# Rounding a weight block by block, and a wider spacing of the last ternary layers, in a two-layer gated cross-attention kernel

## The chip, the cores and the metric

The kernel runs on one core of a Trainium2 chip, in one launch. The metric is the device time of one execution in microseconds; the figure of a kernel is the median of its runs. The core has five engines that run side by side and wait for each other through semaphores: PE (matrix products and transposes), DVE (vector), ACT (scalar functions), POOL (general vector work) and SP, whose queue issues all transfers here. Results of PE lie in PSUM banks until DVE or ACT has read them.

## The reference

The input `x` is 4 batches of 512 rows of 512, `ctx_2048` has the same shape. Each stage adds a gated term to `x`, and each starts from a layer norm of the current `x`:

```python
x = x + tanh(g_xattn[0]) * wkv(w, u, layernorm(x), ctx_2048)      # a recurrence along the rows
x = x + tanh(g_ffn[0])   * ffn(layernorm(x), w1, w2, w3)          # weights sign(w)*mean|w|, inputs int8 in groups of 64
x = x + tanh(g_xattn[1]) * attention(layernorm(x), ctx_2048, ...) # 16 heads; wq, wp and rows int8
x = x + tanh(g_ffn[1])   * ternary(layernorm(x), gamma, W)        # W rounded to -1, 0, 1; rows int8
```

Int8 here means for a weight row: `s = max(max|row| / 127, 1e-8)`, and `round(row / s)` clipped to plus and minus 127. The ternary weight is `round(W / (mean|W| + 1e-5))`, clipped to plus and minus 1. The ternary layer's rows pass a layer norm, then a root of a mean square, gamma, and an int8 rounding by their largest magnitude.

## The kernel before, in words

The four batches go through the four stages one behind the other, and the stages of neighbouring batches run beside each other: while batch b's FFN or attention keeps PE busy, batch b+1's recurrence (`wkv_layer`) fills DVE, ACT and POOL, and batch b-1's ternary layer goes between. Everything is cut into generators, and each `yield` ends a step. `line` (L1239) gives a generator a place in time for its steps, in batches and slots (a batch is 17 slots; in the first, `at_unit(n)` counts sixteenths of the FFN), and `run` always takes the step with the smallest place. A `line` with `(start, end, n)` spreads n steps evenly; an `event` is a single step.

That order alone does not settle the program. PE's instructions keep it from turn to turn: `in_turn` ties every product to the last one of the turn before, `next_turn` ends a turn, and within a turn a scheduler may shift. On DVE, ACT, POOL and SP the scheduler places instructions as it finds them ready in its own estimate, so that an earlier place of a step shifts rows of other steps too. Each engine then runs its list strictly in order.

In the first batch the weights are prepared beside FFN (`class Weights`). `load` fetches a weight of 512 x 512 as four blocks of 128 rows into `wn` (two buffers). For the attention's `wq` and `wp`, `rounded` (L407) takes the largest magnitudes of all four blocks in one instruction (`absmax`, L249), the scales and their reciprocals (`int8_scale`, L259 and L260), and then rounds each block with three instructions (`quantise`, L253 to L255: scale, clip and add a large constant, subtract it), into `wi`. For the ternary weight, `ternary_sums` (L421) sums magnitudes, and `ternary` (L430) forms the mean on PE and rounds the four blocks. `ints_turned` then transposes a weight on PE into PSUM (`wt_ps`, sixteen transposes, four to a bank) and copies it out on DVE and ACT in turn. `output_scales` (L448) turns the scales of `wp` into a row on PE (`pb_ps`), multiplies by the gate on DVE (`swp_b`, L457) and fetches and scales the output bias. In the first batch's PSUM, two banks of tag `m` serve all transposes and batch 3's keys and values (`k_ps`, `v_ps`), so a bank that DVE has not yet read holds up PE.

In the stage around it, FFN's unit on PE is: a product `ff_hp`, a second `ff_hp`, a product `ff_acc`, and four transposes `tp_ps`. Between these stand DVE's L761, L765 (gate), L249, L691, L693, L695 (group rounding) and L712 (`hr`), ACT's L760, L699 and L711, and POOL's L700.

Batch 2's ternary layer lies beside batch 3's attention, and batch 3's is the very end. For both, `statistics` (L1130) takes the moments of the rows and forms the inverse root by a seed and three Newton steps: `rsqrt` on DVE (eleven small instructions, L185 to L195), or `rsqrt_aside`, with the seed on DVE (L202, L204) and twelve instructions on POOL (L209 to L213). Batch 3's tiles go in two pairs, (0, 1) and (2, 3); before the change the first pair's root is formed on DVE and the second's on POOL. `ternary` (L1147) then does for a tile: `tf_xn` (L1158), its largest magnitude (L249), the scales (L1162 to L1176), the rounding on ACT (L264), four transposes (`qr_ps`), a copy to `tf_xT` (ACT L271), four products `f_ps`, and the sum into `xb` (DVE L1189) and out. `tf_xn` has three buffers (tag `ff_a`) for four tiles, so that the fourth waits for the first's transposes. Attention's unit (one head pair, 256 rows) on PE is: two `s_ps`, `o_ps`, eight transposes `pt_ps`, two `s_ps`, eight `pt_ps`, and `ot_ps`; on DVE four maxima (L962), two copies `at_PT` (L982), a reciprocal and `at_o` (L1022).

## Time and profile before

| | us |
|---|---|
| median of 3 runs | 1123.73 (1122.61 to 1124.41) |
| the profiled execution | 1121.98 |
| its span | 1120.2 |
| busy: PE, DVE, ACT, POOL | 960.3, 886.3, 711.5, 297.8 |
| mean granted PE clock | 0.954 |

The page lists busy times of each engine, the span in 40 slices, the transfers, the chain of work that ended last, and groups of instructions by line with the engine's idle time before them and what ended it. A row of a timeline gives start, duration, engine, line, operation, output and inputs, and in brackets the idle time before it and who ended that. Rows of one engine overlap by a little, so the time from one start to the next is what an instruction costs in a row of others. PE's clock is granted between 0.5 and 1.0 of full speed, and it shows in the duration of the same product in different places.

### The profile page before, as it was taken

The page shows a single profiled execution, that of the slowest core. Times are in us where ns is not written, and L with a number is a line of the kernel's source. Part 1 is how long each engine was busy: PE and PEld are TensorE (multiplying, and loading weights), DVE is VectorE, ACT ScalarE, POOL GpSimd, SP SyncE. Part 2 cuts the span into 40 slices and gives each one's busy share as a digit, 9 for nine tenths or more (in the row PEclk, how much of TensorE's full clock was granted, in tenths as well). Part 3 has the DMA queues.
Part 4 walks back from the last instruction along what each step waited for, and adds up shares of the span by engine and source line. Part 5 has one row for each costly group of instructions (what it writes and reads, how often), then busy time and mean ns, then how long its engine had stood idle before and what let it go on. Part 6 is the DMA issues. An engine that isn't in the chain of part 4 may idle for free.

```text
span 1120.2 us, 16509 instructions
## 1 busy us (share of the span) xinstructions
PE 960.3 (86%) x5520; PEld 678.2 (61%) x5548; DVE 886.3 (79%) x1884; ACT 711.5 (64%) x1454; POOL 297.8 (27%) x301
## 2 busy tenths in 40 slices
PE   3879898978878978899998797999999899788983
PEld 3345565555546756677776475777777677555651
DVE  5887447778877799998759899977689766689866
ACT  5657655453214677667768676687676677887762
POOL 3822014333104143541215536212122400100000
PEclk8889999998888999999999999999999899999997
DMA  8188953544434664654655555464564563243401
GB/s 281 39 274 321 322 203 129 178 169 153 148 122 151 224 191 157 200 178 163 205 188 184 164 168 181 142 220 157 181 227 156 181 201 110 89 134 109 123 11 38
DMA packets 85668, 189.58 MB, mean 169 GB/s; under 512 B 12240, under 2 KB 36816, under 8 KB 74576
## 3 DMA queue, kind: packets, MB, share of 16 engines
q1 hardware_dynamic: 85584, 188.53, 50.2%
q8 instruction: 44, 0.72, 0.3%
q14 instruction: 40, 0.33, 0.1%
HBM read 148.65 MB, written 39.85 MB: 168 GB/s over the span
## 4 chain that ended last, share of the span: by engine, by line
PE 46%; DVE 28%; ACT 12%; issue 5%; DMA 5%; POOL 3%; SPq 1%; POOLq 0%; ACTq 0%; DVEq 0%
PE ff_hp L168 13%; PE ff_acc L168 6%; PE pt_ps L171 6%; PE o_ps L168 4%; PE v_ps L168 3%; PE s_ps L168 3%; DVE wk_q L655 3%; DVE at_nm L962 3%; ACT at_P L964 3%; PE k_ps L168 2%; PE tp_ps L171 2%; DVE qg_i L695 2%; PE qr_ps L171 1%; ACT at_PT L984 1%; DVE ff_z L765 1%
## 5 line engine op out<-in xcount | busy, mean ns | idle before, releaser
L168 PE MATMUL ff_hp<-wT,xp 128*128 128x512 f32 x1024 | 270.5, 408 | 3.3 <-ACT at_P L964 2.1
L168 PEld LDWEIGHTS ff_hp<-wT,xp 128*128 128x128 f32 x1024 | 194.3, 193 | 51.3 <-ACT at_P L964 4.4
L964 ACT ACTIVATE at_P<-s_ps,at_nm 128x512 f32<-128x512 f32 x256 | 174.5, 689 | 61.8 <-DVE at_nm L962 61.4
L962 DVE TENSOR_REDUCE at_nm<-s_ps 128x1 f32<-128x512 f32 x256 | 166.0, 677 | 28.4 <-PE s_ps L168 28.0
L700 POOL TENSOR_TENSOR ff_z<-qg_b,qg_s 128x512 f32<-128x512 bf16 x64 | 71.1, 1111 | 381.1 <-ACT qg_b L699 328.4
L171 PE MATMUL pt_ps<-ident,at_P 128*128 128x128 f32 x1024 | 141.3, 278 | 11.7 <-ACT at_os L1004 5.2
L984 ACT COPY at_PT<-pt_ps 128x512 f32<-128x512 f32 x224 | 124.7, 595 | 38.1 <-PE pt_ps L171 37.5
L171 PEld LDWEIGHTS pt_ps<-ident,at_P 128*128 128x128 f32 x1024 | 113.2, 141 | 53.1 <-issue 13.8
L168 PE MATMUL ff_acc<-wT,hr 128*128 128x512 f32 x512 | 136.6, 408 | 6.3 <-DVE hr L712 3.3
L168 PE MATMUL s_ps<-at_kR,at_qR 128*128 128x512 f32 x256 | 98.1, 449 | 21.9 <-ACT at_P L964 14.6
L168 PEld LDWEIGHTS ff_acc<-wT,hr 128*128 128x128 f32 x512 | 92.4, 190 | 27.3 <-DVE hr L712 4.6
L760 ACT ACTIVATE ff_z<-ff_hp,coef 128x512 f32<-128x512 f32 x64 | 43.9, 686 | 67.2 <-PE ff_hp L168 65.2
L168 PE MATMUL o_ps<-at_PT,at_V 128*32 128x256 f32 x1024 | 72.0, 395 | 1.3 <-DVE hr L712 0.7
L699 ACT CAST qg_b<-qg_i 128x512 bf16<-128x512 int8 x80 | 49.4, 618 | 36.7 <-DVE qg_i L695 24.6
L168 PE MATMUL v_ps<-wkvT,cT 128*128 128x512 f32 x128 | 65.9, 664 | 5.3 <-DVE wT L336 2.3
L765 DVE SCALAR_TENSOR_TENSOR ff_z<-ff_hp,coef,ff_z 128x512 f32<-128x512 f32 x64 | 47.6, 744 | 27.9 <-PE ff_hp L168 27.8
L168 PEld LDWEIGHTS s_ps<-at_kR,at_qR 128*128 128x128 f32 x256 | 45.7, 193 | 39.4 <-ACT at_P L964 23.8
L761 DVE SCALAR_TENSOR_TENSOR ff_z<-ff_z,ff_hp 128x512 f32<-128x512 f32 x64 | 43.4, 679 | 24.2 <-ACT ff_z L760 24.0
L168 PE MATMUL k_ps<-cT,wkvT 128*128 128x512 f32 x128 | 59.3, 613 | 3.1 <-ACT cT L479 1.4
L711 ACT CAST hr<-tp_ps 128x512 fp32r<-128x512 f32 x64 | 37.6, 587 | 35.7 <-PE tp_ps L171 35.7
L655 DVE RECIPROCAL wk_q<-wk_q 128x256 f32<-128x256 f32 x32 | 54.3, 1718 | 1.4 <-POOL wk_p L643 1.4
L171 PE MATMUL tp_ps<-ident,ff_z 128*128 128x128 f32 x256 | 41.2, 286 | 14.4 <-ACT at_PT L984 5.3
(190 smaller groups left out, 1735.7 us busy)
## 6 DMA issues: line engine op xcount, KB each, us to landing
wT<-wD SPq DMA_DIRECT2D x72, 1024.0 KB, 5.2
wn<-in_L_ffn_w_dram SPq DMA_DIRECT2D x18, 1024.0 KB, 6.8
at_kR<-kD SPq DMA_DIRECT2D x128, 128.0 KB, 3.0
at_qR<-qD SPq DMA_DIRECT2D x256, 64.0 KB, 2.2
wD<-wT SPq DMA_DIRECT2D x12, 1024.0 KB, 5.0
kD<-k_half SPq DMA_DIRECT2D x16, 512.0 KB, 3.3
qD<-at_half SPq DMA_DIRECT2D x32, 256.0 KB, 2.1
cn<-in_ctx_dram SPq DMA_DIRECT2D x8, 512.0 KB, 5.9
```

What stands on the lines that cost most here:

```text
L168: return in_turn(nc.tensor.matmul(*args, **kwargs))
L171: return in_turn(nc.tensor.transpose(*args))
L655: nc.vector.reciprocal(half, half)
L699: nc.scalar.copy(qb, qi)
L700: nc.gpsimd.tensor_tensor(grouped(src), grouped(qb), s.unsqueeze(2).to_broadcast([P, NG, GS]), ALU.mult)
L711: nc.scalar.copy(part[:, 0, :], pt)
L760: nc.scalar.activation(z, hp, AF.Tanh, scale=coef[:, 0:1])
L761: nc.vector.scalar_tensor_tensor(z, z, 1.0, hp, ALU.add, ALU.mult)
L765: nc.vector.scalar_tensor_tensor(z, hp, coef[:, 1:2], z, ALU.mult, ALU.mult)
L962: nc.vector.tensor_reduce(nm, sp, AX.X, ALU.max, negate=True)
L964: nc.scalar.activation(lanes[k, i, t], sp, AF.Exp, bias=nm, accum_out=sums[k][:, t, i : i + 1],)
L984: made[k] = nc.scalar.copy(dst, blocks(pt))
```

## The change

Six edits, in two places of the program. In the first batch: `rounded` takes each block's maximum, scale and reciprocal by itself, rounds the block, and ends a step there; `ternary` ends a step after each rounded block; their steps are spread over 0.6 to 0.8 units, starting 0.2 units earlier; the transposes start 0.05 units later; and `output_scales` comes at unit 13.75 instead of 14.7. In the last batches: the fourth tile's `tf_xn` takes a buffer of the recurrence (`wk_o`); the two pairs of batch 3 exchange the engines of their roots; and the seven steps of batch 2's ternary layer spread over 9.8 slots instead of 7.

```diff
         def rounded(self, key):
...
-            absmax(am, wn)
...
-            int8_scale(s, r, am)
-            wi = self.pool.tile([P, NC, D], BF16, name="wi", tag="sg", bufs=2)
+            self.ints[key] = wi = self.pool.tile([P, NC, D], BF16, name="wi", tag="sg", bufs=2)
             for j in range(NC):
-                quantise(wi[:, j, :], wn[:, j, :], r[:, j : j + 1], -127.0)
-            self.ints[key] = wi
+                at = slice(j, j + 1)
+                absmax(am[:, at], wn[:, j, :])
+                int8_scale(s[:, at], r[:, at], am[:, at])
+                quantise(wi[:, j, :], wn[:, j, :], r[:, at], -127.0)
+                yield
...
             for j in range(NC):
                 quantise(wi[:, j, :], wn[:, j, :], rf, -1.0, 1.0)
-            self.ints["f"] = wi
+                yield
...
-        y = rsqrt_aside(v, n) if b == NB - 1 and tiles[0] else rsqrt(v, n)
+        y = rsqrt_aside(v, n) if b == NB - 1 and not tiles[0] else rsqrt(v, n)
...
-            xn = ff.tile([P, D], F32, name="tf_xn", tag="ff_a", bufs=3)
+            if t == NT - 1:
+                xn = wk.tile([P, T + 1], F32, name="tf_xn", tag="wk_o")[:, 0:D]
+            else:
+                xn = ff.tile([P, D], F32, name="tf_xn", tag="ff_a", bufs=3)
...
-                event(at_unit(load + 1.2), made.ternary)
+                line(made.ternary(), (at_unit(load + 1.0), at_unit(load + 1.6), 4))
             else:
-                event(at_unit(load + 1.0), lambda key=key: made.rounded(key))
-            line(made.ints_turned(key), (at_unit(load + 1.6), at_unit(load + 2.4), 4))
-        event(at_unit(14.7), made.output_scales)
+                line(made.rounded(key), (at_unit(load + 0.8), at_unit(load + 1.6), 4))
+            line(late(lambda key=key: made.ints_turned(key)), (at_unit(load + 1.65), at_unit(load + 2.45), 4))
+        event(at_unit(13.75), made.output_scales)
...
-                else (end + 4.85 / SLOTS, end + 11.85 / SLOTS, 7),
+                else (end + 4.85 / SLOTS, end + 14.65 / SLOTS, 7),
```

The built order of the changed kernel differs from the old one in three stretches of DVE, PE and ACT: the rounding of the three weights, batch 2's ternary layer, and the end. DVE has 18 instructions more (six maxima, six scales, six reciprocals); no engine has any other in number.

More of the change, by code (lines that the diff above doesn't have):

```diff
@@ L438, in ternary @@
             nc.vector.reciprocal(rf, mf)
-            wi = self.pool.tile([P, NC, D], BF16, name="wi", tag="sg", bufs=2)
+            self.ints["f"] = wi = self.pool.tile([P, NC, D], BF16, name="wi", tag="sg", bufs=2)
             for j in range(NC):
                 quantise(wi[:, j, :], wn[:, j, :], rf, -1.0, 1.0)
-            self.ints["f"] = wi
+                yield
         def ints_turned(self, key):
```

## The prediction

> **What bounds the kernel now.** I read the page first (PE 86% of the span, DVE 79%; the chain of work that ended last is PE 46%, DVE 28%, ACT 12%), then placed the edits: the weights' rounding (rows of `w_am`, `wn`, `wi`) runs from 238.7 to 318 us, batch 2's ternary layer from 1017.8 to 1057 us beside batch 3's attention, and the last pairs from 1092 us to the end. In each I read the windows, PE's waits, and the timelines of PE and DVE. PE's waits between 228 and 350 us (us in total, times, longest):

> ```profile
> PE wt_ps L171 <- DVE swp_b L457: 5.1, 1, 5.1
> PE wt_ps L171 <- DVE k_half L291: 4.3, 3, 3.6
> PE tp_ps L171 <- DVE wT L336: 3.5, 1, 3.5
> ```

> All three wait for DVE: the first while twelve instructions of `ternary` stand in a row (313.40 to 317.84), the second behind the whole-tile maximum, the third behind rounding. Three DVE rows of this stage (start, duration):

> ```profile
> 238.70 2.29 DVE L249 TENSOR_REDUCE w_am<-wn 128x4 f32<-128x2048 f32 x1 [0.62 <-DMA wn<-in_L_xattn_wq_dram]
> 271.39 0.42 DVE L254 TENSOR_SCALAR wn<-wn 128x512 f32<-128x512 f32 x1
> 276.07 1.45 DVE L254 TENSOR_SCALAR wn<-wn 128x512 f32<-128x512 f32 x1
> ```

> The first is what is cut in four. The other two are one instruction, 0.42 us alone and 1.45 us beside POOL's `wk_q` L650 (275.15 to 277.23). Batch 2's ternary layer, on PE and in the windows (PE, PEld, DVE, ACT, POOL busy, clock):

> ```profile
> 1031.05 0.93 PE L171 MATMUL qr_ps<-ident,tf_xn 128*128 128x128 f32 x4 [2.75 <-ACT tf_xn L264]
> ...
> 1032.76 1.94 PE L168 MATMUL o_ps<-at_PT,at_V 128*32 128x256 f32 x16
> ...
> 1039.52 1.07 PE L168 MATMUL o_ps<-at_PT,at_V 128*32 128x256 f32 x16
> ```

> ```profile
> 1020.00:1030.00 10.00, 7.14 (x56) 4.86 (x54) 10.00 (x36) 7.82 (x21) 0.00 (x0) 1.00 0.47 137
> 1040.00:1050.00 10.00, 9.79 (x81) 6.60 (x75) 8.04 (x15) 7.86 (x21) 0.00 (x0) 1.00 0.47 146
> ```

> PE stands 2.75 us before the first tile's transposes, with attention's next unit queued behind, while DVE is full; after it `o_ps` takes 1.94 us instead of 1.07. The end:

> ```profile
> 1103.41 0.19 POOL L209 TENSOR_TENSOR rs_t<-ln_v,rs_y 128x2 f32<-128x2 f32 x1 [137.65 <-DVE rs_y L204]
> ...
> 1106.49 0.19 POOL L213 TENSOR_TENSOR rs_y<-rs_y,rs_t 128x2 f32<-128x2 f32 x1
> ```

> ```profile
> 1107.41 0.81 ACT L264 ACTIVATE tf_xn<-tf_xn,magic,tf_s 128x512 f32<-128x512 f32 x1 [1.92 <-DVE tf_s L1171]
> 1108.13 1.24 ACT L271 ACTIVATE tf_xT<-qr_ps,magic 128x512 bf16<-128x512 f32 x2
> ```

> POOL's roots of the second pair take 3.3 us; ACT's rounding of that pair waits for them, and the first pair's copies `tf_xT` stand behind it.

> **Part 1, rounding (forecast -2.5 us).** The order of instructions of the two kernels, from the first `w_am` to the last `wi`, is priced by start-to-start time between neighbours that wait for nothing: reduce or copy of 512 elements 0.60, `L253` 0.40, `L254` and `L255` 0.34, scan 1.14, half reciprocal 1.66, small ones 0.07 to 0.11. Before, this gives 65.5 us of the 79.1 between 238.70 and 317.84; idle rows add 0.90+0.33+1.42+2.39+1.11+1.27+0.19+0.21 = 7.8; the other 5.8 are mostly rows stretched beside POOL (L695 1.20, L660 1.31, L255 1.21, L647 1.77, L254 1.45, L193 1.00: 4.9 over their usual).

> Added: eight maxima of 0.60 for two of 2.20 (+0.4), twelve more scales and reciprocals (+0.9). Moved ahead of the end: `swp_b` (+0.66) and one `hr` (+0.60); behind it, one batch-norm row and small ones (-0.9). So 67.2. What is saved is idle time, as PE's feeders on DVE (`k_half`, `wT`, `hr`) stand earlier. At 251.77 PE waits for `k_half` with 1.6 us less ahead of it. PE's `tp_ps` of 282.15 comes some 4 us sooner by hand: the rows between the scan at 271.73 and the `wT` copy that it waits for come to 4.6 us instead of 6.5, and the scan stands 1.9 sooner. So the 2.39 us that DVE idles behind a `v_ps` at low clock (6.71 us for 3.45; granted 0.72 from 285 to 295) goes, and I take 1.3 from the smaller ones. Idle 4.1, stretched rows as before: 238.7 + 67.2 + 5.8 + 4.1 = 315.8. PE's `wt_ps` of 318.63 needs no `swp_b` any more: 316.0, 2.6 sooner, rounded to 2.5. What is late next: `wpT`'s transposes. By the order, the third weight's sums (2.20) stand ahead of the second's last block, so PE waits some 4 us near 293, a wait that before lacks. Ends: no idle at all, 311.7, PE at 311.9 (-6.7); idle as before and eight more stretched rounding rows (two of 36 before, 0.92 over each, 7.3), 326.8, PE at 327.0 (+8.4).

> From 345 us to 1017 us PE, DVE and ACT have the same order in both, so I carry the shift. Costed at nothing: the load of batch 3's `xb` on SP passes behind a `kD` and a `wD` store (278.68, 279.14, 282.07) and lands 6.6 us after issue; the first FFN of batch 1 hides it, else 3.4 us. One POOL memset (0.10) changes places with an `ff_z`; ACT's `wk_xn` passes one copy; `bp_b`'s load and product stay early in both orders.

> Row first: L254 0.42 alone, 1.45 beside POOL. [...]

> **Part 2, batch 2's ternary layer (forecast -3.0 us).** Steps stand 1.4 slots apart instead of 1.0, and the fourth tile has a row of its own. PE's units (starts of their first `s_ps`: 1022.32, 1031.63, 1038.77, 1044.96, 1051.16, 1056.91, 1062.35, 1067.67, 1073.43) take 9.31, 7.14, 6.19, 6.20, 5.75, 5.44, 5.32, 5.76. DVE's part of a unit is 4x0.60 + 2x0.60 + 0.3 = 3.9; a tile adds 0.65 + 0.60 + 0.4, later 0.67. Before, three tiles and the roots stand ahead of the second unit's maxima (1032.60). After, two do (1.9 less), and the transposes of the first stand behind that unit's scores: PE goes from `ot_ps` (end 1028.1) straight on, 3.5 us sooner. Then DVE has 2.0 to 2.3 us beside its 3.9 in two units, and PE 1.3 us of transposes and products in three: by hand the seven units are 6.35, 5.4, 5.9, 6.3, 6.6, 5.4, 6.2, together 42.15, so 1028.1 + 42.15 = 1070.25 where before has 1073.43: 3.2 sooner. I take 3.0, as the third and fourth tile stand together on DVE. Ends: the whole wait and the slow rows behind it (0.87+0.49+0.32), -4.4; DVE is full to 1041 either way, so 0, or +1 if the two tiles hold up a unit.

> **Part 3, the end (forecast -0.5 us).** First pair on POOL: seed at 1097.90, twelve POOL instructions 3.3, so 1101.3 instead of DVE's 1103.25. But DVE, in order, stands from 1099.6 to 1101.3, and the second pair's statistics wait behind. First rounding on ACT at 1102.0 (before 1103.98), second pair's `ln_v` done 1103.8 (before 1101.7). Its roots on DVE have two `xb` L1189 in their midst, which wait for `f_ps`: the second's end lies at 1107.5 with PE at full clock, at 1108.4 with half. Nine steps less three already done at 0.2, then 0.7 of scales: ACT's rounding at 1110.0 to 1111.0. Before, PE had f_ps until 1112.45 and the tail followed at 3.6 to the last `xb`. From 1110.0 at full clock 4.1 give 1114.1 (-1.9); from 1111.0 at half clock 6.4 give 1117.4 (+1.3). PE stands some 2.5 us before it, and 2.75 at 1028 sufficed for slow rows, so I stay near the middle: -0.5.

> **Sum.** -2.5 - 3.0 - 0.5 = -6.0. The profiled execution took 1121.98 (span 1120.2), so 1116.0; it lies 1.75 under the median of the runs shown, 1123.73, and against that the forecast is **1117.7**.

> **Rivals.** *DVE was the bound in the rounding all along*: idle time only changes places. For it: DVE is 76 to 100% busy in every window from 245 to 315. Part 1 gives 0, time 1120.2. Chance 0.18.

> *Stretched rows*: the roundings strewn beside POOL's products of `wkv_layer` (1.26 to 2.14 each, ten between 244 and 281) stretch by 0.92, eight more than before, on FFN's own path, so that no idle goes: part 1 +8.4, with the rest +4.9, time 1128.6, slower. It decides from a loss over 3.5 + 2.25 us in part 1. Against it: before, two of 36 met. Chance 0.14.

> *Part 2 gives nothing*, DVE being full there in either order, and part 1 half: 1122.0. Chance 0.10.

> *PE keeps its clock* between 270 and 330, near both ends of parts 1 and 2: -6.7 - 4.4 - 0.5 = -11.6, 1112.1. Chance 0.08.

> Forecast as summed, between 1114 and 1120: 0.50.

> **Chances.** 0.2% (2.25 us) is about what a measurement of this kernel can tell from no change. Faster takes the forecast, the clock case and most of the first rival: 0.69. Same takes its rest and the third: 0.16. Slower: 0.15. The range for 8 in 10 runs from 1111.5 to 1126.5; outside are the worse part of the stretched rows and a little of the clock case.

> **What would show it.** Part 1: the `wt_ps` wait of 5.1 under 4.5 and the attention's first `qr_ps` (348.60) near 346; a new wait before `wpT`'s transposes. Part 2: no wait of 2.75 before the first `tf_xn` transposes, the unit after 1022 near 6 instead of 9.3. Part 3: POOL's twelve at about 1098 relative to before, DVE idle 1.7 us, the first pair's `tf_xT` two to four us sooner. Wrong: L253 to L255 rows of 1.2 us in number, a new PE gap near 293 over 6 us, or DVE idle as long as before.

## The result, and the profile after

The changed kernel takes **1125.32 us** (median of 22 runs, 1120.24 to 1127.76); the kernel before, on the same chip, 1122.63 us (22 runs, 1116.02 to 1127.99). The ratio is 1.0026 (95% interval 1.0015 to 1.0038): slower by some 3 us, where 6 us less were forecast. The profiled execution took 1126.90 us, its span is 1125.1, its mean granted clock 0.951.

First the rounding. PE's waits of the changed kernel between 228 and 350 us (us in total, times, longest), to be held against the three of before:

```profile
PE wt_ps L171 <- DVE wi L255: 7.7, 5, 2.0
PE tp_ps L171 <- DVE wT L336: 2.8, 1, 2.8
PE wt_ps L171 <- DVE k_half L291: 2.8, 1, 2.8
```

The one long wait for `swp_b` (5.1) is gone, those for `k_half` and `wT` are shorter (4.3 and 3.5 before), and five waits for rounded blocks, 7.7 us together, are new. Two of the five stand before the second weight's transposes. Rows of DVE and, below, of PE in that place:

```profile
296.44 2.28 DVE L428 TENSOR_REDUCE w_part<-wn 128x64 f32<-128x2048 f32 x1
298.63 0.42 DVE L255 TENSOR_SCALAR wi<-wn 128x512 bf16<-128x512 f32 x1
...
300.60 0.43 DVE L255 TENSOR_SCALAR wi<-wn 128x512 bf16<-128x512 f32 x1
```

```profile
299.11 0.23 PE L171 MATMUL wt_ps<-identb,wi 128*128 128x128 bf16 x1 [1.97 <-DVE wi L255]
301.09 0.23 PE L171 MATMUL wt_ps<-identb,wi 128*128 128x128 bf16 x1 [1.75 <-DVE wi L255]
```

The third weight's sums (`w_part`, 2.28 us) run on DVE ahead of the second weight's last two blocks, and PE stands 3.7 us for these. The other three waits (4.0 us) stand before the third weight's transposes. On DVE the stretch from the first `w_am` to the last `wi` takes 79.6 us (before 79.2), with 7.2 us idle (before 8.0); the same list of instructions takes 81.4 us, 8.8 of them idle, in the profile of the rounding edits alone. Two of the rounding rows are stretched beside POOL (1.20 and 1.07 us), as two were before.

Batch 2's ternary layer, PE rows and two windows (PE, PEld, DVE, ACT, POOL busy, clock):

```profile
1037.77 0.50 PE L168 MATMUL s_ps<-at_kR,at_qR 128*128 128x512 f32 x1 [0.98 <-ACT at_P L965]
1038.10 0.60 PE L171 MATMUL qr_ps<-ident,tf_xn 128*128 128x128 f32 x4
...
1042.02 1.07 PE L168 MATMUL o_ps<-at_PT,at_V 128*32 128x256 f32 x16 [1.35 <-ACT at_PT L985]
```

```profile
1020.00:1030.00 10.00, 8.88 (x72) 5.47 (x73) 9.84 (x28) 7.10 (x19) 0.00 (x0) 1.00 0.70 194
1040.00:1050.00 10.00, 8.48 (x75) 5.44 (x74) 9.55 (x26) 8.09 (x20) 0.00 (x0) 1.00 0.11 31
```

PE no longer stands before the first tile's transposes (2.75 us before), and is busier from 1020 to 1030 (8.88 of 10 us, before 7.14); from 1040 to 1050 it is less busy (8.48, before 9.79), since waits of about 1 us for ACT's `at_P` and `at_PT` come instead. The changed program stands 5.4 us later here; windows shifted by that (1025.4 to 1035.4, 1045.4 to 1055.4) have 9.04 and 8.33. The units from the third's first `s_ps` to the start of the last one's `o_ps` take 60.3 us, before 61.9.

The end, rows of POOL, DVE and ACT:

```profile
1101.78 0.20 POOL L209 TENSOR_TENSOR rs_t<-ln_v,rs_y 128x2 f32<-128x2 f32 x1 [130.47 <-DVE rs_y L204]
...
1105.28 0.20 POOL L213 TENSOR_TENSOR rs_y<-rs_y,rs_t 128x2 f32<-128x2 f32 x1
```

```profile
1105.51 0.33 DVE L1166 TENSOR_SCALAR tf_s<-tf_s,rs_y 128x1 f32<-128x1 f32 x2 [2.03 <-POOL rs_y L213]
```

```profile
1106.21 1.52 ACT L264 ACTIVATE tf_xn<-tf_xn,magic,tf_s 128x512 f32<-128x512 f32 x2 [9.55 <-DVE tf_s L1175]
...
1114.54 1.52 ACT L264 ACTIVATE tf_xn<-tf_xn,magic,tf_s 128x512 f32<-128x512 f32 x2 [4.77 <-DVE tf_s L1175]
```

POOL takes 3.7 us, DVE stands 2.03 us for it (before, 2.58 us for the second pair's), and ACT rounds the second pair 8.3 us after the first. From the last unit's `o_ps` to the end of the span it is 42.3 us, before 41.2.

The profile after thus has -1.7 us in the rounding, up to attention's second `qr_ps` (349.73 before, 349.52 after), -1.6 in the units and +1.1 at the end. The rest of its 4.9 us lies where the programs are the same: 1.5 ahead of the first edit, and 5.6 between that `qr_ps` and the units in batch 3's attention (first `s_ps` 1017.10 before, 1022.49 after). Whether the change does that, or the execution that was profiled, the two traces cannot say.

### The profile page after: what moved, and what is told of

Its sections match the earlier page's. It is cut to its first block, busy times and chain, and to the rows that moved or that the text cites. A ratio compares the mean times of both kernels' runs of the same rounds, so it can differ in the third digit from the quotient of the medians.

```text
span 1125.1 us, 16520 instructions
## 1 busy us (share of the span) xinstructions
PE 965.0 (86%) x5520; PEld 682.7 (61%) x5548; DVE 888.2 (79%) x1902; ACT 711.5 (63%) x1454; POOL 297.8 (26%) x301
## 4 chain that ended last, share of the span: by engine, by line
PE 47%; DVE 27%; ACT 14%; issue 5%; DMA 4%; POOL 3%; SPq 0%; ACTq 0%; POOLq 0%; DVEq 0%
PE ff_hp L168 14%; PE ff_acc L168 6%; PE pt_ps L171 6%; PE s_ps L168 4%; PE o_ps L168 4%; ACT at_P L965 4%; PE v_ps L168 3%; DVE wk_q L656 3%; DVE at_nm L963 2%; DVE qg_i L696 2%; PE k_ps L168 2%; PE tp_ps L171 2%; ACT at_PT L985 2%; PE qr_ps L171 2%; PE f_ps L168 2%
## 5 line engine op out<-in xcount | busy, mean ns | idle before, releaser
L168 PE MATMUL ff_hp<-wT,xp 128*128 128x512 f32 x1024 | 275.6, 413 | 2.8 <-ACT at_P L965 2.1
L168 PEld LDWEIGHTS ff_hp<-wT,xp 128*128 128x128 f32 x1024 | 198.7, 197 | 52.1 <-ACT at_P L965 4.6
L171 PE MATMUL pt_ps<-ident,at_P 128*128 128x128 f32 x1024 | 142.8, 280 | 10.3 <-ACT at_os L1005 4.9
L171 PEld LDWEIGHTS pt_ps<-ident,at_P 128*128 128x128 f32 x1024 | 114.7, 142 | 51.2 <-issue 15.2
L168 PE MATMUL ff_acc<-wT,hr 128*128 128x512 f32 x512 | 138.9, 413 | 6.2 <-DVE hr L713 4.0
L168 PE MATMUL s_ps<-at_kR,at_qR 128*128 128x512 f32 x256 | 99.2, 452 | 22.5 <-ACT at_P L965 15.7
L168 PEld LDWEIGHTS ff_acc<-wT,hr 128*128 128x128 f32 x512 | 94.2, 193 | 27.1 <-DVE hr L713 5.0
L168 PE MATMUL o_ps<-at_PT,at_V 128*32 128x256 f32 x1024 | 70.8, 389 | 2.0 <-ACT at_PT L985 2.0
L168 PEld LDWEIGHTS s_ps<-at_kR,at_qR 128*128 128x128 f32 x256 | 46.0, 194 | 40.2 <-ACT at_P L965 25.2
L168 PE MATMUL v_ps<-wkvT,cT 128*128 128x512 f32 x128 | 64.0, 648 | 5.5 <-DVE wT L336 2.3
L168 PE MATMUL k_ps<-cT,wkvT 128*128 128x512 f32 x128 | 59.9, 618 | 3.1 <-ACT cT L480 1.4
L171 PE MATMUL tp_ps<-ident,ff_z 128*128 128x128 f32 x256 | 39.8, 278 | 14.7 <-ACT at_PT L985 4.9
```

The lines of the kernel that those rows point to most:

```text
L168: return in_turn(nc.tensor.matmul(*args, **kwargs))
L171: return in_turn(nc.tensor.transpose(*args))
```

## The experiments

Two theories to begin with. *Middle*: the rounding edits bring the loss behind 350 us. *Tail*: that loss is scatter, and the exchanged roots make the kernel slower. Ratios are to the kernel before, with 95% intervals; us are these ratios times 1123.3.

**Each part alone.** *Roots alone*:

```
-        y = rsqrt_aside(v, n) if b == NB - 1 and tiles[0] else rsqrt(v, n)
+        y = rsqrt_aside(v, n) if b == NB - 1 and not tiles[0] else rsqrt(v, n)
```

> The kernel before with the exchanged roots alone: last batch's first pair on POOL, second pair on DVE; the program is the same up to some 1092 us. Theory 'middle' (the changed kernel's loss is the 5.7 us that its trace loses between 350 and 1011 us, brought by the rounding edits, and the end adds about what its trace shows): the end, from the last o_ps to the end of the span, is 42.3 us instead of 41.2, time +0.5 to +1.5 us against the kernel before. Theory 'tail' (the 5.7 us are scatter of one execution, the exchange is what makes the kernel slower): +3 to +6 us.

Measured 1.0022 (1.0005 to 1.0038), +2.5 us, in neither theory's range. The end takes 42.6 us, 1.4 more than before. And its profile loses 5.1 us between the same second `qr_ps` and the units, where it is the program of before to the instruction: so two profiles of one program differ by 5 us there.

*Spacing alone*, with the fourth tile's buffer:

```
-                else (end + 4.85 / SLOTS, end + 11.85 / SLOTS, 7),
+                else (end + 4.85 / SLOTS, end + 14.65 / SLOTS, 7),
```

> The kernel before with the wider spacing of batch 2's ternary layer and the fourth tile's own row buffer alone. Both theories: from the third unit's first s_ps to the last o_ps 60.3 us as in the changed kernel instead of 61.9, time -1 to -2 us against the kernel before. If the gain of 1.6 us seen there comes from the other start of the stage and not from the spacing: 0.

Measured 0.9993 (0.9975 to 1.0012), -0.8 us. The units take 60.3 us, 1.6 less, as in the changed kernel; the end takes 42.1 us, 0.9 more. So about half of what the units gain is given back at the end.

*Rounding edits alone*, all that the diff has in the first batch:

```
+                line(made.rounded(key), (at_unit(load + 0.8), at_unit(load + 1.6), 4))
...
+        event(at_unit(13.75), made.output_scales)
```

> The kernel before with the rounding edits alone: block by block in four steps, sooner, output scales at 13.75. Theory 'middle': PE's first ff_hp after wfT's transposes comes 1 to 2 us sooner than before (relative to the stage's start), and 4 to 6 us are lost between 350 and 1011 us: +2 to +4 us against the kernel before. Theory 'tail': the gain of 1.5 us stays, -1 to -2 us.

Measured 1.0033 (1.0015 to 1.0051), +3.7 us. *Rounding edits and spacing*, which is the change without this line:

```
+        y = rsqrt_aside(v, n) if b == NB - 1 and not tiles[0] else rsqrt(v, n)
```

> The changed kernel with the roots as before (rounding edits and spacing together). Theory 'middle': +1 to +2.5 us against the kernel before. Theory 'tail': -2 to -4 us.

Measured 1.0027 (1.0009 to 1.0046), +3.0 us; with the exchanged roots, which is the whole change, +2.9. So the loss is the rounding edits' in all three, the *tail* theory falls, and beside the spacing the exchange costs nothing that can be told. Why it measured +2.5 by itself stays open.

**Which of the rounding edits.** New pair of theories: *late blocks* (the second weight's last block behind the third's sums) against *strewn* (more instructions between others). *wq and wp in steps alone*:

```
-                event(at_unit(load + 1.0), lambda key=key: made.rounded(key))
+                line(made.rounded(key), (at_unit(load + 0.8), at_unit(load + 1.6), 4))
```

> Of the rounding edits, those to wq and wp alone: both block by block in four steps, their transposes 0.05 units later; the ternary weight and the output scales as before. Theory 'late blocks' (the blockwise rounding gains some 2 us up to the first weight's transposes, and gives them back before the second weight's, as the second's last block now stands behind the third's sums of 2.28 us on DVE and PE waits 3.7 us for wi there): the 3.7 us stand in PE's waits, the 5.1 for swp_b too, time +2 to +4 us against the kernel before. Rival 'strewn' (eighteen more instructions, and roundings stretched between others, cost it wherever they stand): +1.5 to +2.5 us, with no change if the 3.7 us wait is absent.

Measured 1.0016 (0.9995 to 1.0037), +1.8 us, which is in the range of *strewn* and just under that of *late blocks*; the two waits stand (wi 3.7, swp_b 4.5). *The ternary weight in steps, output scales at 13.75, alone*:

```
-                event(at_unit(load + 1.2), made.ternary)
+                line(made.ternary(), (at_unit(load + 1.0), at_unit(load + 1.6), 4))
...
-        event(at_unit(14.7), made.output_scales)
+        event(at_unit(13.75), made.output_scales)
```

> Of the rounding edits, the ternary weight in four steps and the output scales at 13.75 alone; wq and wp as before, so that no wait before wp's transposes comes. Theory 'late blocks': the swp_b wait of 5.1 us goes, one for wi of at most 4.0 us in two or three pieces comes in its place, time -1 to -2 us against the kernel before. Rival 'strewn': +1 to +2 us.

Measured 1.0000 (0.9984 to 1.0016). The wait for swp_b goes and 3.8 us for wi come, yet there is neither gain nor loss, as neither theory had it. *Output scales alone*, the last two lines of that diff:

> The output scales at 13.75 instead of 14.7 alone. Both theories: swp_b (0.66 us on DVE) leaves the end of the third weight's rounding, PE's wait there is for wi, 4.4 instead of 5.1 us: -0.5 us, within what the comparison can tell. If the product of the output bias or the earlier pb_ps transposes hold up another unit: +1 us.

Measured 1.0005 (0.9987 to 1.0022): nothing. *All rounding edits, steps sooner*:

```
-                line(made.ternary(), (at_unit(load + 1.0), at_unit(load + 1.6), 4))
+                line(made.ternary(), (at_unit(load + 0.9), at_unit(load + 1.2), 4))
...
-                line(made.rounded(key), (at_unit(load + 0.8), at_unit(load + 1.6), 4))
+                line(made.rounded(key), (at_unit(load + 0.6), at_unit(load + 1.0), 4))
```

> All rounding edits, but the steps sooner: those of wq and wp from 0.6 to 1.0 units behind the load instead of 0.8 to 1.6, the ternary's from 0.9 to 1.2 instead of 1.0 to 1.6. On DVE the last block of wp then stands ahead of the third weight's sums. Theory 'late blocks': the wait for wi before wp's transposes falls from 3.7 us to under 1, time -1 to -2.5 us against the kernel before. Rival 'strewn': +3 to +4 us as with all rounding edits.

Measured 0.9946 (0.9924 to 0.9968), **-6.1 us**, with the same added instructions. PE's waits of this kernel from 228 to 350 us (us in total, times, longest):

```profile
PE wt_ps L171 <- DVE k_half L291: 3.9, 2, 3.0
PE tp_ps L171 <- DVE wT L336: 3.5, 1, 3.5
...
PE wt_ps L171 <- DVE wi L255: 1.4, 1, 1.4
```

The waits for wi fall from 7.7 to 1.4 us, and DVE's stretch of rounding takes 74.5 us, instead of 81.4 with the edits where the change has them. *Strewn* falls. But the 6.3 us of waits give 9.8 between this kernel and the one with the edits as the change places them: more than *late blocks* expected.

**Place or steps.** *No steps, only sooner*:

```
-                event(at_unit(load + 1.2), made.ternary)
+                event(at_unit(load + 0.9), made.ternary)
...
-                event(at_unit(load + 1.0), lambda key=key: made.rounded(key))
+                event(at_unit(load + 0.6), lambda key=key: made.rounded(key))
...
-        event(at_unit(14.7), made.output_scales)
+        event(at_unit(13.75), made.output_scales)
```

> No steps: each weight is rounded whole as in the kernel before, only sooner (wq and wp 0.6 units behind the load instead of 1.0, the ternary 0.9 instead of 1.2), the transposes at 1.65, the output scales at 13.75. Theory 'place' (the time is set by where the last block of a weight stands ahead of its transposes on DVE; steps are beside the point): about the 6.1 us of the early steps, -4 to -7 us against the kernel before. Rival 'steps' (the blocks in steps let PE's feeders through, and that is what the early steps gain by): -1 to -3 us, with waits for k_half, wT or swp_b as long as before (4.3, 3.5, 5.1 us).

Measured 0.9979 (0.9958 to 1.0001), -2.4 us, with `k_half` 5.6 and `wT` 3.5 us as expected of *steps*. *wq's and wp's steps sooner, the ternary's as in the change*, only the second pair of lines of the diff of the early steps:

> All rounding edits, with the steps of wq and wp sooner (0.6 to 1.0), those of the ternary weight where the change has them (1.0 to 1.6). Theory 'place': the wait for wi before wp's transposes (3.7 us) is gone, the one before wf's (4.0) stays; time 3.5 to 4.5 us less than with all rounding edits, 0 to -2 us against the kernel before. Rival: the ternary's place is what matters alone, +2 to +4 us.

Measured 0.9977 (0.9962 to 0.9992), -2.6 us; wi 4.0 us. So neither the place nor the steps do it alone. *Early steps and spacing*, and, behind it, *the whole change with early steps*, each with the four lines of that diff:

> The early steps together with the wider spacing of batch 2's ternary layer and its row buffer; roots as before. -6.1 of the early steps and -0.8 of the spacing alone: -6 to -8 us against the kernel before. If the spacing only moves work to the end: -5 to -6 us.

Measured 0.9944 (0.9924 to 0.9963), -6.3 us.

> The whole change with the early steps: differs from the kernel with early steps and spacing by the exchanged roots alone. By the run of the roots alone (+2.5 us) -4 to -5 us against the kernel before; by the ends of the traces (42.3 us against 42.1 to 42.9 with the spacing and the old roots) the same as without the exchange, -6 to -8 us.

Measured 0.9931 (0.9905 to 0.9957), **-7.8 us**, 1116.58: below both kernels and the best ratio of all, though its interval overlaps those of the other two with early steps. Again the exchange costs nothing beside the spacing.

**Where the loss lies.** Programs cut off at a place. Up to their last rows PE, DVE and ACT have the order of the whole programs; POOL lacks two memsets, and SP's transfers differ somewhat, alike in every cut:

```
-    run(NB + 9)
+    run(1.25)
+    for b in range(NB):
+        nc.sync.dma_start(out=out[b].rearrange("(t p) d -> p t d", p=P), in_=xs[0])
```

> The kernel before, cut off at place 1.25 (after the first q_ps of batch 0's attention, some 375 us); the rest is left out, and the outputs are batch 0's rows as they then stand, written four times. It is the base for the other three: some 385 to 400 us.

> The rounding edits alone, cut off at the same place; the rest is left out. If the loss is made in the rounding stage: +2 to +4 us against the cut kernel before. If the stage gains or is even, and the loss is made behind it (by where the clock's low stretches fall, or by the runs that were taken): -2 to +0.5 us.

> The early steps, cut off at the same place; the rest is left out. If the stage makes the gain: -5 to -8 us against the cut kernel before, and 7 to 10 less than the cut rounding edits.

> The steps of wq and wp alone, cut off at the same place; the rest is left out. Theory 'late blocks': the 3.7 us wait before wp's transposes and the 4.5 for swp_b both stand, +2 to +3 us against the cut kernel before. Rival: 0 to +1.

Medians of 4, 5, 4 and 4 runs: 386.54 (385.95 to 387.25), **384.61** (383.69 to 385.69), 377.67 (376.16 to 380.86), 386.27 (383.71 to 388.55). So in the stage itself the rounding edits gain 1.9 us, in ranges that do not touch, and the early steps 8.9. The steps of wq and wp alone gain 0.3, where *late blocks* had +2 to +3. Behind the cut the edits then lose 3.7 + 1.9 = 5.6 us, and the early steps 2.8.

The profiles say less. ACT's first `at_xn` stands at 346.0 to 348.7 us (mean 347.8) in the five profiles without any rounding edit (before, its two cuts, roots alone, spacing alone), at 346.4 to 349.7 (348.0) in the five that have them as the change does, and at 340.5 to 342.4 (341.2) in the four with early steps. By these the stage gains nothing and the early steps 6.6 us, so that they would lose little behind it (-6.1 at the end). The stage's gain thus lies between nothing and 2 us; that the edits do not lose 3.7 us in it holds by both. So *late blocks* falls as the cause of the loss: the waits it named are there, but with them the stage does not lose. Cut off at place 2.1, with `xs[1]` written out (here a few rows of DVE, ACT and POOL in the last 100 us are missing too):

> The kernel before, cut off at place 2.1 (behind batch 1's FFN, some 600 us); the rest is left out, and the outputs are batch 1's rows as they then stand, written four times. The base for the next: 590 to 620 us.

> The rounding edits alone, cut off at place 2.1; the rest is left out. If the 5.6 us go lost within batch 1's FFN and the recurrence beside it: +2.5 to +4.5 us against the cut kernel before. If they go lost later, or are spread over all batches: -2 to +1 us.

Medians 558.57 (556.77 to 561.02, 4 runs) and 562.39 (557.17 to 564.40, 5 runs): +3.8, the whole kernel's loss, though the ranges overlap. So by the medians all of it arises between 386 and 558 us, in batch 1's FFN: 172.0 us before, 177.8 with the edits (the two cuts were timed on different chips).

What differs there? Windows of the cut kernel before and, below, of the cut one with the rounding edits, which stands 3.6 us later in its execution (columns as above). The one is the profile of the fastest run of its kernel (556.77), the other of the slowest (564.40), so they show more than the medians' difference:

```profile
400.00:420.00 20.00, 16.43 (x103) 13.03 (x103) 18.26 (x29) 14.36 (x30) 8.08 (x9) 1.00 0.65 209
420.00:440.00 20.00, 17.14 (x113) 12.64 (x112) 19.96 (x30) 12.45 (x29) 10.31 (x10) 1.00 0.46 157
```

```profile
400.00:420.00 20.00, 15.35 (x81) 11.43 (x80) 17.47 (x25) 11.76 (x26) 11.50 (x10) 0.91 0.66 213
420.00:440.00 20.00, 17.12 (x101) 13.54 (x100) 19.14 (x29) 12.25 (x27) 9.36 (x10) 0.93 0.41 147
```

The granted clock is 1.00 against 0.91 and 0.93. The rows show where it falls. PE of the kernel before, then of the whole kernel with the rounding edits alone, each at the same three units:

```profile
408.25 0.94 PE L168 MATMUL s_ps<-at_kR,at_qR 128*128 128x512 f32 x2 [2.17 <-ACT at_P L964]
409.03 2.00 PE L168 MATMUL ff_hp<-wT,xp 128*128 128x512 f32 x8
...
434.73 0.94 PE L168 MATMUL s_ps<-at_kR,at_qR 128*128 128x512 f32 x2 [1.88 <-ACT at_P L964]
435.51 2.02 PE L168 MATMUL ff_hp<-wT,xp 128*128 128x512 f32 x8
...
460.47 0.95 PE L168 MATMUL s_ps<-at_kR,at_qR 128*128 128x512 f32 x2 [2.07 <-ACT at_P L964]
461.24 3.58 PE L168 MATMUL ff_hp<-wT,xp 128*128 128x512 f32 x8
```

```profile
409.27 1.08 PE L168 MATMUL s_ps<-at_kR,at_qR 128*128 128x512 f32 x2 [2.19 <-ACT at_P L965]
410.16 3.46 PE L168 MATMUL ff_hp<-wT,xp 128*128 128x512 f32 x8
...
437.05 1.23 PE L168 MATMUL s_ps<-at_kR,at_qR 128*128 128x512 f32 x2 [1.88 <-ACT at_P L965]
438.08 3.19 PE L168 MATMUL ff_hp<-wT,xp 128*128 128x512 f32 x8
...
464.21 1.23 PE L168 MATMUL s_ps<-at_kR,at_qR 128*128 128x512 f32 x2 [2.07 <-ACT at_P L965]
465.24 3.26 PE L168 MATMUL ff_hp<-wT,xp 128*128 128x512 f32 x8
```

The same wait for ACT (2.2, 1.9, 2.1 us, 26 to 28 us apart) is followed by products at full clock twice and at half clock once in the one, and at half clock three times in the other. The trace records the granted clock in steps: every stretch at half clock is 3.41 us long or a multiple (3.41 to 13.65 us in the profiles of before and after), and within an execution all of them begin on one grid of 3.413 us. I took, in each profile, how far past a grid line the first of these waits (at 400 to 410 us) ends, the steps at half clock in the stretch from 8 us before that to 102 us behind it, and the time to a mark (a `pt_ps` behind a wait for `at_os`) some 110 us on:

| profile | us past the line | half-clock steps | us to the mark |
|---|---|---|---|
| no steps, only sooner | 1.18 | 1 | 107.6 |
| wq, wp early | 1.57 | 2 | 109.5 |
| before, cut at 2.1 | 1.60 | 2 | 108.1 |
| before | 1.61 | 2 | 108.0 |
| output scales alone | 1.70 | 3 | 110.0 |
| early steps | 1.76 | 3 | 110.0 |
| wq, wp in steps alone | 1.80 | 3 | 110.0 |
| early steps and spacing | 1.81 | 3 | 109.9 |
| whole change, early | 1.93 | 3 | 110.3 |
| spacing alone | 1.94 | 3 | 110.3 |
| ternary in steps alone | 2.44 | 4 | 112.3 |
| rounding edits alone | 2.78 | 4 | 112.2 |
| rounding edits and spacing | 2.85 | 4 | 112.2 |
| the whole change | 2.86 | 4 | 112.2 |
| rounding edits, cut at 2.1 | 2.90 | 4 | 112.2 |
| roots alone | 3.19 | 4 | 111.9 |

From 107.6 to 112.3 us for one and the same list of instructions: the steps rise in the order in which the wait lies on the grid, without an exception, and the time rises with them. All four profiles with the rounding edits where the change has them are among the six longest. Before and its cut are among the three shortest, but the spacing and the roots, with the program of before up to there, lie at 1.94 and 3.19. With the same number of steps, programs with and without the edits take the same time (112.2 and 111.9; 110.0 and 110.3).

The same traces show it wait by wait. Cut every wait of PE of more than 1.2 us in this stretch at the grid lines, which gives 136 pieces that lie between two lines at full clock. Of the 85 pieces under 1.70 us none was followed by a half-clock step at the next line; of the 51 from 1.70 us on 49 were (not: one of 1.72 and one of 1.85). So a wait of 2.2 us that ended 1.61 us past a line was followed by no step at the next, and those that ended 1.70 or 2.8 past were.

*What stays open.* That a wait's place on the grid sets these steps is read from sixteen profiles; no kernel that only shifts the later program was tried. Nor is it shown why the rounding edits arrive late on the grid so often (2.8 to 2.9 us past a line in four profiles of four, against one of four, at 3.19, without any rounding edit). And the 5.6 us carry the intervals above: some 3 to 8.

Nor need the steps be the whole loss. The granted clock on record for every run gives its steps: the share of clock lost times the span, 1.71 us for each. From the first cut to the second the kernel before has 1.7 steps on average, and 4.1 with the edits. At 1.0 us a step (the slope over 109 runs of the kernel before) to 1.7 (the slope in the table), these 2.4 steps are 2.4 to 4.1 of the 5.6 us. The whole kernel has 33.5 steps with the rounding edits alone, against 32.1 before on the same chip, which is 1.4 to 2.4 of the 3.7 us; but the whole change, 2.9 us slower, has 32.5 against 32.3 (over those 109). So more steps go with a part of the loss, and the rest has no cause shown.

## Why the prediction was wrong

**The step that failed**: "From 345 us to 1017 us PE, DVE and ACT have the same order in both, so I carry the shift." The order is the same, but the shift is not carried: by the cut kernels -1.9 us at 386 us are +3.8 at 558. By the profiles the shift at 348 us is about nothing; then too the loss arises behind, where nothing was edited. With no loss there the sum of what was measured would be 0 to -1.9 (rounding) - 0.7 (spacing with its end), at best -2.6.

*Part 1, -2.5.* Not far off by the cut kernels, -1.9; too much by the profiles, which show no gain. Its mechanism was half right. The `wt_ps` wait for `swp_b` went; the new wait before `wpT`'s transposes came (forecast some 4 us near 293, found 3.7 at 299 to 301), and `tp_ps` came 3.8 us sooner from the first `w_am` on (forecast 4). But I had DVE's idle time fall from 7.8 to 4.1 us and the last block 2 us sooner; idle fell to 7.2 and the last block did not move (79.2, then 79.6 us from the first `w_am`). Rows of PE of the cut kernel before and, below, of the cut one with the edits show what differs instead:

```profile
318.88 3.76 PE L168 MATMUL ff_hp<-wT,xp 128*128 128x512 f32 x8
322.44 4.52 PE L168 MATMUL v_ps<-wkvT,cT 128*128 128x512 f32 x8
```

```profile
318.34 3.46 PE L168 MATMUL ff_hp<-wT,xp 128*128 128x512 f32 x8
321.63 3.60 PE L168 MATMUL v_ps<-wkvT,cT 128*128 128x512 f32 x8
```

Behind the one wait of 5.1 us the clock is at half for 6.8 us, behind the three short ones for 3.4; so the edits are 0.5 us ahead at `ff_hp` and 1.7 at the next `tp_ps` (331.32 and 329.58). That is read from one pair of profiles and was not tried apart. I also took the new wait as a price that was paid within the sum and did not ask what it would be worth to avoid it: steps 0.1 to 0.6 units earlier gave 6.9 us more in the stage, by the cut kernels and by the profiles.

*Part 2, -3.0.* Mis-sized: -0.8 measured. The wait of 2.75 us went as forecast, but the units gained 1.6, not 3 (`ot_ps` ended at 1028.30, not at 1028.1 as I read it, which takes 0.2 off the 3.2): waits of PE for `at_P` rose from 1.9 to 3.0 us and one of 1.35 for `at_PT` came. The end of the span then returned 0.9, a term that I did not have.

*Part 3, -0.5.* Each event came as put down: POOL 3.3 us (3.7 found, one row 0.64 instead of 0.2), DVE standing 1.7 (2.03), two `xb` rows amid the root's chain, a clock at half behind PE's gap (3.43 us, forecast 2.5). They sum to +1.4 at the end alone and to nothing beside the spacing. The run of the roots alone gave +2.5; 1.4 is what its end shows, and the rest lies within the interval.

*Rivals.* Stretched rows beside POOL: two rounding rows before (1.21 and 1.45 us), two after (1.20 and 1.07); not it, and no run here shows that they cost the change anything. DVE the bound all along: closer than the forecast for DVE's own list, but the stage did not lose by it. None of the rivals had a later stage give the gain back. And the profile of before, from which I took the carry, is one of the three shortest in the table.

## What to carry to other kernels

When an edit shifts everything behind it, do not carry the shift through stages in which PE waits regularly for some 2 us: cut the program behind the edited stage and time both parts, since two profiles of one program can differ by more than the effect. When work is split to be overlapped, see that its last piece does not come later than the whole did, and ahead of whom it stands; here the same split placed 0.1 to 0.6 units sooner turned +2.9 into -7.8 us.
